# Block 1's tokens turned on VectorE and by DMA instead of on TensorE, the first loads reordered, and later sums moved to other places

## The chip, the cores and the metric

The kernel runs on one core of a Trainium2 chip. The core has five engines with an instruction queue each. TensorE (PE) multiplies matrices into PSUM. VectorE (DVE) and ScalarE (ACT) read and write PSUM and SBUF. GpSimd (POOL) works on SBUF alone. SyncE (SP) issues DMAs here, and ACT's queue issues some as well. Every queue is served in order: an instruction that waits holds up all those behind it on the same engine. The metric is the device time of one execution in microseconds (us).

## The reference

`x` is two samples of 2048 tokens with 512 features, `t` one condition vector of 512 for each sample. Everything is float32.

```python
emb = jnp.dot(jax.nn.silu(t), ada_w) + ada_b
shift_msa, scale_msa, gate_msa, shift_mlp, scale_mlp, gate_mlp = jnp.split(emb, 6, axis=-1)
norm = _ln(x) * (1.0 + scale_msa[:, None]) + shift_msa[:, None]
h = jax.nn.gelu(jnp.dot(norm, ssm_w1) + ssm_b1, approximate=False)
ssm_out = jnp.dot(h, ssm_w2) + ssm_b2
x = x + gate_msa[:, None] * ssm_out
norm2 = _ln(x) * (1.0 + scale_mlp[:, None]) + shift_mlp[:, None]
hf = jax.nn.gelu(jnp.dot(norm2, ff_w1) + ff_b1, approximate=True)
ff_out = jnp.dot(hf, ff_w2) + ff_b2
x = x + gate_mlp[:, None] * ff_out
```

`ssm_w1` and `ssm_w2` are 512x512, `ff_w1` is 512x1024, `ff_w2` 1024x512, and `ada_w` 512x3072, in six column groups `ada_0` to `ada_5`.

## The kernel before, in words

The 4096 tokens are cut into 8 blocks of 512 (`x_0` to `x_7`, 1 MB each). Each block goes through four stages: `hA` (the first ssm product and its gelu, class `First`), `oA` (the second ssm product, added into the block, `residual`), `hC` (first product of the feed-forward part, class `Second`) and `oC` (its second product). The stages of different blocks are interleaved by hand: after the start, PE's order is hA 0, oA 0, hA 1, oA 1, hC 0, hA 2, oC 0, hC 1 and so on, up to oA 6, hA 7, oC 5 and the end with block 7.

Each stage's product is done in the Strassen-Winograd way: seven products P1 to P7 of half-size matrices in place of eight, at the price of sums of the operands' quarters made beforehand (`sums_of_first`, `sums_of_second`: four operations s0, s1, a difference in place, and s2). A product is 8 matmuls of 128x128 with 256 columns. The seven gather in three PSUM banks: P1, P6, P7 and P4 share bank "y", P5 and P3 bank "v", P2 has "x". Every product that adds into a bank has to wait until the product before it in that bank has been read by DVE or ACT. The order of the seven is an argument: `ORDER` is P1 P2 P6 P5 P7 P3 P4, `FIRST` is P1 P2 P5 P6 P7 P3 P4, `CARRIED` is P1 P5 P6 P2 P7 P3 P4. The `hooks` of a stage are operations that are emitted after one of its products. They sit in the queues of their own engines in this order; with `CARRIED` the names of the places are those of `ORDER`, counted by position.

Before a block can be multiplied, it is normalized (mean and variance by `stats`, then `scales` on POOL, eight operations of four elements per partition, then `normal`), transposed so that features lie on partitions, and modulated with scale and shift. There are two ways of transposing. On PE: `turned` lets PE transpose 16 squares of 128x128 and modulates out of PSUM. By DVE and DMA: `turn` (DVE transposes 32x32 blocks, four operations), `move` (16 DMAs of 64 KB that carry the 32-row pieces between partitions) and `moved` (ACT modulates in place, four operations). Blocks 0 and 1 use PE for their first norm, all others the second way.

At the start SP issues the loads in the order x_0 (two halves), ada_0, ada_1, w1, ada_2, w2, the row of gate bias (`load_gate_b(2)`, four small DMAs), b2, x_1, ada_3, ada_4, fw1, and after block 0's first sums ada_5, fw2, `load_gate_b(5)`. The DMAs take eight semaphores in turn, so that each issue waits for the landing of the eighth DMA before it. `modulation(g0, part)` and `gate_rows_of(g)` multiply the condition with one ada group on PE (32 small matmuls into `pada`, line L275); DVE takes the result. `first_ssm_gate` spreads the ssm gate over the partitions (`pgate`, L310), and `fold2` multiplies w2 with it (four DVE operations, L396) and makes w2's four sums on POOL (L348). `seed` copies a bias row into a PSUM bank on ACT before the products add to it; block 0 has instead four POOL additions of the bias to `x_0` (`biases`, L752).

Of the kernel before, what the change touches and what calls it, by code (L numbers as in the profile page):

```python
# [36 lines left out]
F32 = mybir.dt.float32  # L37
# [103 lines left out]
def kernel(  # L141
# [16 lines left out]
    nc = tc.nc  # L158
# [100 lines left out]
    load_gate_b(2)  # L259
    b2_bc = work.tile([P, D], F32, tag="gb", name="gb2_0", bufs=2)  # L260
    load_row(b2_bc, b2)
    load_x(1)
    load_ada(3)
    load_ada(4)
    fw1_sb = load_w("fw1", fw1)

    mods = {}

# [224 lines left out]
    def hook(hooks, places, ops):  # L493

        for n, op in enumerate(ops):
            hooks.setdefault(places[min(n, len(places) - 1)], []).append(op)


    class Norm:
# [6 lines left out]
        def stats(self):  # L506
# [98 lines left out]
        def transpose(self, k, pt=None):  # L605
            if pt is None:
                pt = ps_t.tile([P, TB], F32, tag="t", name=f"pt{self.name}_{k}")
            for c in range(C):
                nc.tensor.transpose(
                    pt[:, c * P : (c + 1) * P], self.xn[:, c, k * P : (k + 1) * P], ident  # L610
                )
            return pt

# [31 lines left out]
        def summed(self, eng, in_big=False):  # L645

            if in_big:
                flat = big_tile(f"nS{self.name}").rearrange("p a b -> p (a b)")[:, : 3 * KD // 2 * HT]
                s = thirds(flat.rearrange("p (s a k r) -> p s a k r", s=3, a=C, k=KD // 2))
            else:  # L650
                s = thirds(sums.tile([P, 3, C, KD // 2, HT // C], F32, tag="s", name=f"nS{self.name}"))
            h = self.nT.rearrange("p a (k h r) -> p a k h r", k=KD, h=2)
            lo, hi = h[:, :, : KD // 2], h[:, :, KD // 2 :]
            q = {
                "11": lo[:, :, :, 0],
                "12": lo[:, :, :, 1],
                "21": hi[:, :, :, 0],
                "22": hi[:, :, :, 1],
            }
            self.ops = second_operands(q, s)  # L660
            return sums_of_second(q, s, eng)

    def hidden(name, rhs, wops, bT, func, lo, hi, g, hooks, order=ORDER, on_act=()):

# [262 lines left out]
    class First:  # L927
# [201 lines left out]
    load_ada(5)  # L1129
    fw2_sb = load_w("fw2", fw2)  # L1130
    load_gate_b(5)
    gb, hA = {2: b2_bc}, {}
    found = {}

# [8 lines left out]
        return [lambda k=k: found["w2"][1][k]() for k in range(lo, hi)]  # L1143

    hooks = {}
    hook(hooks, ("P1",), n1_sums[2:3])
    hook(hooks, ("P2",), [lambda: gate_rows_of(2, "grows")] + n1_sums[3:])
    st = n1[1].stats()
    hook(hooks, ("P5",), [ssm_gate, gb2_0] + biases(0, b2_bc) + [lambda: apart_row(b2_bc, nc.gpsimd)] + fold2(0, 1))
    hook(hooks, ("P6",), fold2(1, 7))  # L1150
    hook(hooks, ("P3", "P7"), st[:2])
    hook(hooks, ("P7",), [lambda: modulation(3, 0)])
    hA[0] = First(0, n1[0].ops, hooks, ("P1", "P2", "P5", "P6", "P3", "P7", "P4"), hA_0)
    w2_ops = found["w2"][0]

    hA_sums = hA[0].summed(nc.vector)
    run(hA_sums[:2])
    hooks = {}
    hook(hooks, ("P1",), hA_sums[2:3] + st[2:] + [n1[1].scales] + fold2(7, 8))
    hook(hooks, ("P2",), hA_sums[3:] + [lambda c=c: n1[1].normal(c, on_pe=True) for c in range(C)])  # L1160
    hook(hooks, ("P6",), [lambda: modulation(3, 1)])
    hook(hooks, ("P3", "P3", "P4"), n1[1].turned())
    n2 = {0: Norm(0, 2)}
    st = n2[0].stats()
    hook(hooks, ("P3",), st[:2])
    fw1_ops, fw1_sums, fw1_s = weight_of_first("fw1", fw1_sb)
    hook(hooks, ("P2",), fw1_sums[:1])
    hook(hooks, ("P5", "P4"), fw1_sums[1:3])
    residual("oA_0", 0, hA[0], w2_ops, KD // 2, hooks, order=FIRST)

    def ff_gate():
        take_gate(5, 0)
# [8 lines left out]


    n1_sums = n1[1].summed(nc.vector)
    run(st[2:3] + n1_sums[:2] + st[3:])
    hooks = {}
    hook(hooks, ("P1",), n1_sums[2:3] + [n2[0].scales])
    hook(hooks, ("P2",), n1_sums[3:] + [lambda c=c: n2[0].normal(c) for c in range(C)])
    hook(hooks, ("P5", "P7"), [lambda p=p: seed("oA_1", gb[2], p) for p in range(2)])
    hook(hooks, ("P6",), [lambda: gate_rows_of(5, "g5")])
    hook(hooks, ("P6", "P6", "P7", "P7"), [lambda c=c: n2[0].turn(c) for c in range(C)])  # L1190
    hook(hooks, ("P7",), [lambda: n2[0].move((nc.sync,), (0, 1)), lambda: store_gates(5), lambda: load_gate(5, 0)])
    fb2_bc = work.tile([P, D], F32, tag="gb", name="gb5_0", bufs=2)
# [85 lines left out]
    for i in range(1, NBLK):  # L1278
# [213 lines left out]
```

## Time and profile before

| what | value |
|---|---|
| time, median of 3 runs | 588.19 us (588.06 to 589.07) |
| the profiled execution's own time | 588.16 us |
| its span, first to last instruction | 586.4 us |
| PE busy | 577.9 us, 99% of the span |
| DVE, ACT, POOL busy | 417.9, 263.1, 428.4 us |
| mean granted TensorE clock | 0.999 |

The span is the time from the first to the last profiled instruction; 1.8 us of the time lie around it. A row of the timeline has the start, the length, the engine, the line in the kernel, the operation, output and input tiles, and in brackets the idle time of the engine just before and what ended it. Rows of one kind that follow each other are merged (x8 is eight instructions); the length of a merged matmul row is longer than the distance to the next row, since matmuls overlap: products of 8 follow each other every 1.73 us.

### The profile page before, as it was taken

Reading aid. Unit: us, or ns where it says so; the run is one execution under the profiler, and the core shown is the slowest. Engines: PE = TensorE matmul, PEld = TensorE weight load, DVE = VectorE, ACT = ScalarE, POOL = GpSimd, SP = SyncE. Lnnn points to the kernel's source line nnn. Section 1 sums busy time; section 2 is a strip of 40 time slices with the busy share of each in tenths; the row PEclk is TensorE's granted clock in tenths of the full one; section 3 lists DMA queues with packets and bytes.
Section 4 is the critical chain, followed back from the end, with each engine's and each line's share of the span. In section 5 each row is a group of like instructions: output and inputs, shape, how many; then the busy total and the mean of one; then the engine's idle time right before and its main releaser. Section 6 shows DMA issues by size and latency. Waiting matters only on the chain.

```text
span 586.4 us, 9484 instructions
## 1 busy us (share of the span) xinstructions
PE 577.9 (99%) x3303; PEld 515.5 (88%) x3303; DVE 417.9 (71%) x752; ACT 263.1 (45%) x479; POOL 428.4 (73%) x518
## 2 busy tenths in 40 slices
PE   8999999999999999999999999999999999999997
PEld 5888888888899888998889988898887998899896
DVE  4978788987867375685756857883856366787676
ACT  2234357405642554435742588226663431731420
POOL 2875359999997938969688799998688445369351
PEclk9999999999999999999999999999999999999999
DMA  8990323302205403472033721153030330031002
GB/s 317 395 393 10 91 64 82 108 37 107 55 19 178 129 1 74 113 209 72 3 90 78 282 73 29 45 141 129 19 72 1 106 113 0 1 73 72 2 1 72
DMA packets 25243, 56.49 MB, mean 96 GB/s; under 512 B 4672, under 2 KB 5740, under 8 KB 23532
## 3 DMA queue, kind: packets, MB, share of 16 engines
q1 hardware_dynamic: 21856, 51.67, 27.7%
q10 hardware_dynamic: 3340, 4.22, 3.0%
q8 instruction: 26, 0.43, 0.3%
q14 instruction: 21, 0.17, 0.1%
HBM read 32.80 MB, written 8.40 MB: 70 GB/s over the span
## 4 chain that ended last, share of the span: by engine, by line
PE 91%; DVE 3%; DMA 3%; issue 1%; ACT 0%; SPq 0%; DVEq 0%
PE px_hC L985 10%; PE py_hA L475 9%; PE py_oA L475 9%; PE py_hC L985 8%; PE py_oC L778 8%; PE pv_hC L985 8%; PE pl_oC_P_y L824 8%; PE pl_oC_P_v L824 5%; PE pv_hA L475 4%; PE pv_oA L475 4%; PE pl_oC_P_x L824 3%; DMA ada<-in_L_cond_ada_w_dram 2%; PE py_hC L475 2%; PE py_oC L475 2%; PE px_oA L475 2%; PE px_hA L475 2%
## 5 line engine op out<-in xcount | busy, mean ns | idle before, releaser
L623 ACT ACTIVATE nT<-nT,mod,mod 128x512 f32<-128x512 f32 x32 | 23.4, 803 | 56.2 <-DMA nT<-blocks 40.1
L348 POOL TENSOR_TENSOR hSC<-hClo,hChi 128x512 f32<-128x512 f32 (+1 forms) x16 | 19.7, 1235 | 38.7 <-ACT hChi L980 33.3
L512 DVE BATCH_NORM_STATS2 st<-x 128x6 f32<-128x512 f32 x60 | 40.7, 678 | 5.4 <-DMA x<-in_x_dram 5.2
L923 POOL TENSOR_TENSOR forms<-forms 128x256 f32<-128x256 f32 x56 | 41.8, 746 | 3.3
L985 PE MATMUL py_hC<-forms,fw 128*128 128x256 f32 x168 | 41.0, 380 | 0.0
L1002 DVE TENSOR_TENSOR hClo<-hClo,py_hC 128x512 f32<-128x512 f32 x42 | 28.6, 684 | 15.3 <-ACT hClo L999 9.4
L985 PEld LDWEIGHTS py_hC<-forms,fw 128*128 128x128 f32 x168 | 31.7, 190 | 4.7 <-DVE hClo L1002 0.2
L623 ACT ACTIVATE x<-x,mod,mod 128x512 f32<-128x512 f32 x24 | 17.6, 802 | 32.1 <-DMA x<-blocks 32.1
L591 DVE STREAM_TRANSPOSE blocks<-nT 128x512 f32<-128x512 f32 x32 | 22.2, 705 | 13.5 <-ACT nT L580 13.5
L923 POOL TENSOR_TENSOR forms<-nT,forms 128x256 f32<-128x256 f32 x42 | 30.5, 748 | 1.8 <-PE pl_oC_P_v L824 1.3
L923 POOL TENSOR_TENSOR forms<-nT 128x256 f32<-128x256 f32 x14 | 10.4, 740 | 29.3 <-ACT nT L623 20.4
L1002 DVE TENSOR_TENSOR hChi<-hChi,pv_hC 128x512 f32<-128x512 f32 x35 | 23.2, 681 | 10.4 <-PE pv_hC L985 6.7
L580 ACT ACTIVATE nT<-x,nmr,rstd 128x512 f32<-128x512 f32 x32 | 24.1, 806 | 13.4 <-POOL nmr L566 13.4
L985 PE MATMUL px_hC<-forms,fw 128*128 128x256 f32 x112 | 27.6, 379 | 0.0
L980 ACT ACTIVATE hClo<-hClo,colsT 128x256 f32<-128x256 f32 x56 | 25.3, 498 | 5.0 <-DVE hClo L1002 4.8
L838 DVE TENSOR_TENSOR x<-pl_oC_P_y,x 128x256 f32<-128x256 f32 (+1 forms) x66 | 24.7, 374 | 3.0 <-PE pl_oC_P_y L824 1.3
L475 PE MATMUL py_oA<-w,hA 128*128 128x256 f32 x112 | 26.5, 379 | 0.0
L999 ACT ACTIVATE hChi<-py_hC 128x512 f32<-128x512 f32 x14 | 7.6, 593 | 41.1 <-PE py_hC L985 41.0
L980 ACT ACTIVATE hChi<-hChi,colsT 128x256 f32<-128x256 f32 x56 | 25.1, 496 | 1.9 <-DVE hChi L1002 1.9
L739 DVE TENSOR_TENSOR x<-py_oA,x 128x512 f32<-128x512 f32 x26 | 17.8, 686 | 11.2 <-PE py_oA L475 10.6
L778 PE MATMUL py_oC<-fw_s,hSC 128*128 128x256 f32 x112 | 25.3, 379 | 0.0
L739 DVE TENSOR_TENSOR x<-pv_oA,x 128x512 f32<-128x512 f32 x16 | 11.0, 687 | 20.1 <-PE pv_oA L475 9.0
(339 smaller groups left out, 1796.7 us busy)
## 6 DMA issues: line engine op xcount, KB each, us to landing
x<-in_x_dram SPq DMA_DIRECT2D x13, 1024.0 KB
out_dram<-x SPq DMA_DIRECT2D x14, 512.0 KB
ada<-in_L_cond_ada_w_dram SPq DMA_DIRECT2D x6, 1024.0 KB
x<-blocks SPq DMA_DIRECT2D x96, 64.0 KB
nT<-blocks SPq DMA_DIRECT2D x80, 64.0 KB
fw<-in_L_cond_ff_w_dram SPq DMA_DIRECT2D x2, 2048.0 KB
w<-in_L_cond_ssm_w_dram SPq DMA_DIRECT2D x3, 1024.0 KB
nT<-blocks ACTq DMA_DIRECT2D x48, 64.0 KB
```

The lines of the kernel that those rows point to most:

```text
L475: nc.tensor.matmul(ps[b][j * apart][:, j, :], lhs(p, j, k), rhs(p, j, k), start=(fresh and j * (not apart) == 0 and k == 0), stop=(p in (" ...
L512: nc.vector.bn_stats(st, xs[self.i][:, c, :])
L580: nc.scalar.activation(t, x_c, AF.Identity, bias=self.nmr[:, c : c + 1], scale=self.rstd[:, c : c + 1])
L623: nc.scalar.activation(dst, src, AF.Identity, bias=shift, scale=scale)
L739: nc.vector.tensor_tensor(d, ps[BANK[p]][:, js], d, ALU.add)
L778: yield lambda j=j, k=k: nc.tensor.matmul(ps[BANK[p]][:, j, :], hops(p, j, k), wops[p][:, k, :], start=False, stop=(k == kdim - 1), skip_g ...
L824: nc.tensor.matmul(t[:, n, :], hops.leaves[p][f][:, k, :], leaf_wops[p][f][:, k, :], start=room not in started, stop=(f in ("P2", "P3", "P ...
L838: nc.vector.tensor_tensor(d, src, d, ALU.add)
L923: eng.tensor_tensor(reg[d], reg[a], reg[b], ALU.add if f == "+" else ALU.subtract)
L980: nc.scalar.activation(h, h, AF.Gelu_apprx_tanh, bias=fb1T[:, m : m + 1])
L985: nc.tensor.matmul(ps[b][:, j, :], fa[ra][:, j * P : (j + 1) * P], fb[rb].rearrange("p a (c q) -> p c a q", q=Q), start=(fresh and j == 0) ...
L1002: nc.vector.tensor_tensor(dest(d), dest(d), ps[b], op)
```

## The change

Six things are done. First, `x_1` is loaded right behind `w1`, fw1 comes ahead of ada_3, and ada_4, ada_5, fw2, gate bias 5 are issued behind block 1's moves. Second, block 1 is turned by DVE and DMA: its statistics are taken half by DVE and half by ACT (`stats_shared`) during hA 0, the normals run on ACT, and the moves are issued on SP and ACT at the end of hA 0. Third, block 0's ssm bias is seeded into PSUM; the four POOL additions go. Fourth, in hA 0 the gate's products come after P5 and not after P2, two biases of the hidden layer are added on ACT, three of the four sums of its output go to POOL, and the modulation 3 leaves hA 0 for oA 0 and hA 1; oA 0 runs in `ORDER` in place of `FIRST`. Fifth, the sums of fw1, of block 0's second norm and the folds of fw2 stand at other places or engines. Sixth, for the last block (`ahead`) the four sums of the first norm are made after the fourth and the fifth product of oA 6 and after the first and second of hA 7; before, two came after the third product of oA 6, one after the fourth and one after the fifth. The transposes of block 0 on PE are written as matmuls that open their PSUM bank once.

```diff
     w1_sb = load_w("w1", w1)
+    load_x(1)
     load_ada(2)
...
     load_row(b2_bc, b2)
-    load_x(1)
+    fw1_sb = load_w("fw1", fw1)
     load_ada(3)
-    load_ada(4)
-    fw1_sb = load_w("fw1", fw1)
...
+        def stats_shared(self):
...
+            def on_dve(c):
...
+                nc.vector.bn_stats(st, xs[self.i][:, c, :])
+                nc.vector.bn_aggr(self.mv[:, c, :], st)
+
+            def mean(c):
+                nc.scalar.activation(
+                    unread[:, c], xs[self.i][:, c, :], AF.Identity, scale=1.0 / D, accum_out=self.mv[:, c, :1]
+                )
+
+            def square(c):
+                nc.scalar.activation(
+                    unread[:, c],
+                    xs[self.i][:, c, :],
+                    AF.Square,
+                    bias=less[:, c : c + 1],
+                    scale=half,
+                    accum_out=self.mv[:, c, 1:],
+                )
+
+            first, second = [range(h * C // 2, (h + 1) * C // 2) for h in range(2)]
+            rest = slice(C // 2, C)
+            return [lambda c=c: mean(c) for c in second] + [lambda c=c: on_dve(c) for c in first], [
+                lambda: nc.gpsimd.tensor_scalar(less[:, rest], self.mv[:, rest, 0], -half, None, ALU.mult)
+            ] + [lambda c=c: square(c) for c in second]
...
-        def summed(self, eng):
+        def summed(self, eng, first=None):
...
-            return sums_of_first(q, s, eng)
+            return sums_of_first(q, s, first or eng)[:1] + sums_of_first(q, s, eng)[1:]
...
+    st, squares = n1[1].stats_shared()
+    normals = [lambda c=c: n1[1].normal(c) for c in range(C)]
+    turns = [lambda c=c: n1[1].turn(c) for c in range(C)]
+    hook(hooks, ("P1",), st)
+    hook(hooks, ("P2",), squares + [n1[1].scales] + n1_sums[2:3])
+    hook(hooks, ("P5",), [lambda: gate_rows_of(2, "grows")] + n1_sums[3:])
+    hook(hooks, ("P6",), [ssm_gate, gb2_0, lambda: apart_row(b2_bc, nc.gpsimd)] + fold2(0, 2) + normals)
+    hook(hooks, ("P6", "P4"), [lambda p=p: seed("oA_0", b2_bc, p) for p in range(2)])
+    hook(hooks, ("P7",), turns[:2] + fold2(2, 5))
+    hook(hooks, ("P3",), turns[2:3] + fold2(5, 6))
+    hA[0] = First(0, n1[0].ops, hooks, FIRST, hA_0, ("P1", "P5"))
+    w2_ops = found["w2"][0]
+
+    hA_sums = hA[0].summed(nc.gpsimd, nc.vector)
+    run(hA_sums[:1])
+    n1[1].turn(3)
+    n1[1].move((nc.sync, nc.scalar))
+    load_ada(4)
     load_ada(5)
     fw2_sb = load_w("fw2", fw2)
     load_gate_b(5)
...
-    hook(hooks, ("P1",), n1_sums[2:3])
-    hook(hooks, ("P2",), [lambda: gate_rows_of(2, "grows")] + n1_sums[3:])
-    st = n1[1].stats()
-    hook(hooks, ("P5",), [ssm_gate, gb2_0] + biases(0, b2_bc) + [lambda: apart_row(b2_bc, nc.gpsimd)] + fold2(0, 1))
-    hook(hooks, ("P6",), fold2(1, 7))
-    hook(hooks, ("P3", "P7"), st[:2])
-    hook(hooks, ("P7",), [lambda: modulation(3, 0)])
-    hA[0] = First(0, n1[0].ops, hooks, ("P1", "P2", "P5", "P6", "P3", "P7", "P4"), hA_0)
...
-    run(hA_sums[:2])
+    run(hA_sums[1:2] + fold2(6, 7) + hA_sums[2:])
     hooks = {}
-    hook(hooks, ("P1",), hA_sums[2:3] + st[2:] + [n1[1].scales] + fold2(7, 8))
-    hook(hooks, ("P2",), hA_sums[3:] + [lambda c=c: n1[1].normal(c, on_pe=True) for c in range(C)])
-    hook(hooks, ("P6",), [lambda: modulation(3, 1)])
-    hook(hooks, ("P3", "P3", "P4"), n1[1].turned())
+    hook(hooks, ("P1",), fold2(7, 8))
+    hook(hooks, ("P6",), n1[1].moved())
...
+    hook(hooks, ("P4",), [lambda: modulation(3, 0)])
...
-    hook(hooks, ("P5", "P4"), fw1_sums[1:3])
-    residual("oA_0", 0, hA[0], w2_ops, KD // 2, hooks, order=FIRST)
+    hook(hooks, ("P5",), fw1_sums[1:2])
+    residual("oA_0", 0, hA[0], w2_ops, KD // 2, hooks)
...
-    run(st[2:3] + n1_sums[:2] + st[3:])
+    run(st[2:] + n1_sums[:2])
...
+    hook(hooks, ("P1", "P6"), [lambda: modulation(3, 1), lambda: gate_rows_of(5, "g5")])
...
-    hA[1] = First(1, n1[1].ops, hooks, FIRST)
+    hA[1] = First(1, n1[1].ops, hooks, FIRST, on_act=("P1",))
...
-    n2_sums = n2[0].summed(nc.gpsimd)
-    hook(hooks, ("P5",), n2_sums[:1] + [n1[2].scales])
-    hook(hooks, ("P7",), n2_sums[1:] + [lambda c=c: n1[2].normal(c) for c in range(C)])
-    hook(hooks, ("P7", "P3", "P4"), fold5(0, 3))
+    n2_sums = n2[0].summed((nc.vector, nc.vector, nc.gpsimd, nc.gpsimd))
+    hook(hooks, ("P5",), [n1[2].scales])
+    hook(hooks, ("P7",), n2_sums + [lambda c=c: n1[2].normal(c) for c in range(C)])
+    hook(hooks, ("P7",), fold5(0, 1))
...
             if ahead:
-                hook(hooks, ("P6", "P6", "P5", "P7"), n1[i + 2].summed(nc.vector, True))
+                n1_sums = n1[i + 2].summed(nc.vector, True)
+                hook(hooks, ("P5", "P7"), n1_sums[:2])
...
             if ahead:
                 hooks = {}
+                hook(hooks, ("P1", "P2"), n1_sums[2:])
                 hook(hooks, ("P2", "P6"), oC_seeds)
```

More of the change, by code (lines that the diff above doesn't have):

```diff
@@ L515, in stats @@
             return [lambda c=c: op(c) for c in range(C)]
+        def stats_shared(self):
+            n, half = self.name, D**-0.5
+            self.mv = small.tile([P, C, nc.vector.BN_AGGR_DIM], F32, tag="mv", name=f"mv{n}")
+            unread = work.tile([P, C, D], F32, tag="blocks", name=f"unread{n}")
+            less = small.tile([P, C], F32, tag="less", name=f"less{n}", bufs=1)
+            def on_dve(c):
+                st = small.tile([P, nc.vector.BN_STATS_DIM], F32, tag="st", name=f"st{n}_{c}")
+                nc.vector.bn_stats(st, xs[self.i][:, c, :])
[18 more added lines that the diff above has]
+            ] + [lambda c=c: square(c) for c in second]
         def sums_on_act(self):
@@ L608, in transpose @@
             for c in range(C):
-                nc.tensor.transpose(
-                    pt[:, c * P : (c + 1) * P], self.xn[:, c, k * P : (k + 1) * P], ident
+                nc.tensor.matmul(
+                    pt[:, c * P : (c + 1) * P],
+                    self.xn[:, c, k * P : (k + 1) * P],
+                    ident,
+                    start=(c == 0),
+                    stop=(c == C - 1),
+                    is_transpose=True,
+                    skip_group_check=True,
                 )
@@ L660, in summed @@
             self.ops = second_operands(q, s)
-            return sums_of_second(q, s, eng)
+            engs = eng if isinstance(eng, tuple) else (eng,) * 4
+            return [sums_of_second(q, s, e)[n] for n, e in enumerate(engs)]
     def hidden(name, rhs, wops, bT, func, lo, hi, g, hooks, order=ORDER, on_act=()):
@@ L1128 @@
     run(n1_sums[:2])
-    load_ada(5)
-    fw2_sb = load_w("fw2", fw2)
-    load_gate_b(5)
     gb, hA = {2: b2_bc}, {}
@@ L1145 @@
     hooks = {}
-    hook(hooks, ("P1",), n1_sums[2:3])
-    hook(hooks, ("P2",), [lambda: gate_rows_of(2, "grows")] + n1_sums[3:])
-    st = n1[1].stats()
-    hook(hooks, ("P5",), [ssm_gate, gb2_0] + biases(0, b2_bc) + [lambda: apart_row(b2_bc, nc.gpsimd)] + fold2(0, 1))
-    hook(hooks, ("P6",), fold2(1, 7))
-    hook(hooks, ("P3", "P7"), st[:2])
-    hook(hooks, ("P7",), [lambda: modulation(3, 0)])
-    hA[0] = First(0, n1[0].ops, hooks, ("P1", "P2", "P5", "P6", "P3", "P7", "P4"), hA_0)
-    w2_ops = found["w2"][0]
-    hA_sums = hA[0].summed(nc.vector)
-    run(hA_sums[:2])
+    st, squares = n1[1].stats_shared()
[9 more added lines that the diff above has]
+    hA[0] = First(0, n1[0].ops, hooks, FIRST, hA_0, ("P1", "P5"))
+    w2_ops = found["w2"][0]
+    hA_sums = hA[0].summed(nc.gpsimd, nc.vector)
[3 more added lines that the diff above has]
+    load_ada(4)
+    load_ada(5)
+    fw2_sb = load_w("fw2", fw2)
+    load_gate_b(5)
+    run(hA_sums[1:2] + fold2(6, 7) + hA_sums[2:])
     hooks = {}
-    hook(hooks, ("P1",), hA_sums[2:3] + st[2:] + [n1[1].scales] + fold2(7, 8))
-    hook(hooks, ("P2",), hA_sums[3:] + [lambda c=c: n1[1].normal(c, on_pe=True) for c in range(C)])
-    hook(hooks, ("P6",), [lambda: modulation(3, 1)])
-    hook(hooks, ("P3", "P3", "P4"), n1[1].turned())
+    hook(hooks, ("P1",), fold2(7, 8))
+    hook(hooks, ("P6",), n1[1].moved())
     n2 = {0: Norm(0, 2)}
@@ L1183 @@
     n1_sums = n1[1].summed(nc.vector)
-    run(st[2:3] + n1_sums[:2] + st[3:])
+    run(st[2:] + n1_sums[:2])
     hooks = {}
-    hook(hooks, ("P1",), n1_sums[2:3] + [n2[0].scales])
-    hook(hooks, ("P2",), n1_sums[3:] + [lambda c=c: n2[0].normal(c) for c in range(C)])
+    hook(hooks, ("P1",), n1_sums[2:3] + [n2[0].scales] + fw1_sums[2:])
+    hook(hooks, ("P2",), [lambda c=c: n2[0].normal(c) for c in range(C)])
     hook(hooks, ("P5", "P7"), [lambda p=p: seed("oA_1", gb[2], p) for p in range(2)])
-    hook(hooks, ("P6",), [lambda: gate_rows_of(5, "g5")])
+    hook(hooks, ("P1", "P6"), [lambda: modulation(3, 1), lambda: gate_rows_of(5, "g5")])
     hook(hooks, ("P6", "P6", "P7", "P7"), [lambda c=c: n2[0].turn(c) for c in range(C)])
+    hook(hooks, ("P6",), n1_sums[3:])
     hook(hooks, ("P7",), [lambda: n2[0].move((nc.sync,), (0, 1)), lambda: store_gates(5), lambda: load_gate(5, 0)])
@@ L1205 @@
     hooks = {}
-    hook(hooks, ("P1",), hA_sums[2:3] + fw1_sums[3:])
+    hook(hooks, ("P1",), hA_sums[2:3])
     hook(hooks, ("P2",), hA_sums[3:])
@@ L1224 @@
     hook(hooks, ("P3",), [n2[1].scales])
-    hook(hooks, ("P6", "P5", "P7", "P3", "P4"), fold5(3, 8))
+    hook(hooks, ("P2", "P6", "P5", "P7", "P3", "P4"), fold5(1, 8))
     hook(hooks, ("P4",), [lambda: store_gates(2)])
```

## The prediction

> **What bounds the kernel now.** The page's first part says PE is busy 99% of the span, so only PE's own work and its few waits count. The waits by engine name PE's in the program's body, the chain of waits and PE's timeline place them, and DVE's timeline says why the last one arises. Waits of PE, longest first:
>
> ```profile
> PE py_oA L475 <- DVE x L739: 1.4, 1, 1.4
> PE idle L1078 <- POOL ident masks.py:199: 1.3, 1, 1.3
> PE rowsT L1087 <- DMA fw_t<-in_L_cond_ff_b_dram: 0.7, 1, 0.7
> PE pada L275 <- DMA ada<-in_L_cond_ada_w_dram: 0.7, 2, 0.4
> ```
>
> The first sits in the last blocks; the next two lie ahead of all that is changed. PE's timeline at the start (16 to 29 us), at block 1's transposes and around the long wait:
>
> ```profile
> 16.47 1.89 PE L475 MATMUL px_hA<-nT,w 128*128 128x256 f32 x8
> 18.60 1.08 PE L275 MATMUL pada<-ada,silu 128*32 128x128 f32 x32 [0.25 <-DMA ada<-in_L_cond_ada_w_dram]
> 19.61 1.99 PE L475 MATMUL pv_hA<-nS,w_s 128*128 128x256 f32 x8
> 21.45 1.05 PE L310 MATMUL pgate<-grows,fw_t 128*128 128x128 f32 x8
> 27.61 1.08 PE L275 MATMUL pada<-ada,silu 128*32 128x128 f32 x32
> ...
> 42.19 1.04 PE L609 MATMUL pt<-ident,blocks 128*128 128x128 f32 x8
> 43.06 1.89 PE L475 MATMUL py_oA<-w_s,forms 128*128 128x256 f32 x8
> 44.79 1.04 PE L609 MATMUL pt<-ident,blocks 128*128 128x128 f32 x8
> ...
> 439.55 1.89 PE L475 MATMUL pv_oA<-w,hSA 128*128 128x256 f32 x8
> 442.83 1.99 PE L475 MATMUL py_oA<-w_s,hA 128*128 128x256 f32 x8 [1.39 <-DVE x L739]
> 444.66 1.67 PE L475 MATMUL py_hA<-x,w 128*128 128x256 f32 x7
> ```
>
> A product of 8 takes 1.73 us, start to start. From 439.55 to 442.83 it is 3.28: PE stands 1.55 us ahead of P4 of oA 6. DVE's timeline there:
>
> ```profile
> 437.32 1.50 DVE L348 TENSOR_TENSOR nS<-x 128x512 f32<-128x512 f32 x1 [0.26 <-ACT x L623]
> 438.93 1.57 DVE L348 TENSOR_TENSOR nS<-x,nS 128x512 f32<-128x512 f32 x1
> 440.42 0.68 DVE L739 TENSOR_TENSOR x<-px_oA,x 128x512 f32<-128x512 f32 x1
> 441.02 1.16 DVE L348 TENSOR_TENSOR x<-x 128x512 f32<-128x512 f32 x1
> 442.10 0.68 DVE L739 TENSOR_TENSOR x<-py_oA,x 128x512 f32<-128x512 f32 x1
> ```
>
> P4 goes into the bank that P7 filled by 439.7, and P7's read (442.10) stands behind three of block 7's sums. Nothing else between 46 and 570 us keeps PE waiting.
>
> **The change part by part.** Times are those of the profiled execution (588.16 us, 0.03 under the median of 588.19).
>
> *Transposes gone.* Two groups of 8 (42.19, 44.79) push the products after them by 0.87 and 0.88 us (chain of waits: 42.35 to 43.23, 44.96 to 45.83): -1.75.
>
> *x_1 ahead of ada_2.* SP's timeline issues x_1 at 14.54, ada_3 at 18.58 and ada_4 at 21.27; its waits there are for w1, ada_2 and w2, the eighth DMA before each. So w1 lands at 14.5, ada_2 at 18.56, w2 at 21.26. A megabyte at the page's 395 GB/s takes 2.66; ada_2 took 4.0, and 1.35 of that is a delay that the later loads carry on. With x_1 in between, ada_2 gets about w2's place. Bounds: 14.5 + 2 x 2.66 = 19.85 without the delay, 21.26 with it. I take 21.2, nearest to the row that shows the second place. Now PE's P2 ends at 18.20 and pada starts at 18.60, a wait of 0.40. Then P1, P2 and P5 end at 19.93 and pada waits until 21.25, 1.32: +0.92 (bounds -0.40 and +0.98). x_1 itself comes at 18.5.
>
> *hA 0 afterwards*, PE: pada to 22.26, P6 to 24.18 (1.92 behind a pada, as at 19.68), pgate to 25.07, P7 to 26.80, P3 to 28.53, P4 to 30.26. The 0.16 that PE stands at 28.6 behind DVE's folds go with the new order: -0.16.
>
> *ACT.* Two means (0.61 each from the rows of block 6's first norm, line L524) after x_1 end at 19.8, the table load (1.28) at 21.1, P2's gelu at 21.7, two squares (0.72, L535) at 23.1. P5's biases (0.84) cost nothing, as P3 reads that bank at 26.8. POOL's scales (3.03 from 35.97 to 39.00) end at 26.2, four normals (2.93) at 29.2, the seed (0.57) at 29.8, before P1 of oA 0 at 30.26. So the seed costs nothing; if x_1's chain comes later it does, from 0.5 us on.
>
> *DVE.* The two bn_stats wait for x_1 to 18.5 and end at 20.2; P2's add waits behind them, but its gelu is first used at 30.26. The gate's rows wait for pada, which is there at 22.3. From pgate at 25.2 on DVE has nine operations in a row, 0.60 apart: b2's product, two folds, P7's add, two turns, two folds, P3's add, ending at 30.7. Then ACT's gelu of P3 (0.55) and P4 (0.84) at 32.15. P2 of oA 0 needs P4's, and could have started at 31.99: +0.2 (bounds 0, and 2.0 if two of the nine take 1.5 like 437.32).
>
> *POOL.* Its four bias additions (4.97 in a row) vanish and relieve nothing that PE waits for. New there are hA 0's three sums, between w2's. From 32.1 on: s1 33.4 (P6 wants it at 33.9), w2's and hA's difference 36.0 (P7: 37.4), s2 37.3 (P3: 39.1), w2's s2 38.6 (P4: 40.8), at 1.27 each. Nothing at 1.27; at 1.72, as beside DVE's sums at 31 us, each still comes, with 0.1 to spare.
>
> *Moves.* The last turn ends at 32.7. 16 issues run on SP and ACT, eight each: 5.05 and 5.2 in the rows of block 0's moves. ACT went on 1.66 after the last issue, here at 39.5; the four modulates end at 42.4. ACT stands still for 7 us, which costs nothing, as oA 0 asks nothing of it. hA 1 starts at 45.83 - 0.8 - 1.2 (a pada group with its edge moves behind it) = 43.85 and needs the first two modulates, at 41.0: spare 2.8.
>
> *Loads behind the moves.* SP issues ada_4 at 37.8. x_0's first half took 4.0 for 512 KB, so a megabyte takes 5.3 at most: 43.1. PE wants it at 45.6, spare 2.5. ada_5 45.8, fw2 51.1, gate bias 5 about 51.5 against DVE's need at 53.0. x_2 at 55 is read at 61. fw1, in ada_3's former place, is there before 30; POOL uses it from 39.
>
> *Later sums.* fw1's, block 0's second norm's and the folds of fw2 move among POOL and DVE in stages where PE has no wait. The nearest need is s1 of n2 0 on PE at 74.5, made on DVE by 69: nothing.
>
> *Block 7's sums.* DVE reads P2 at 438.0 (436.10 + 1.89), makes s0 (1.5) to 440.15, reads P7 to 440.85. P4 can start on time at 441.28, spare 0.4. s1 ends at 442.4, wanted at 446.5; the in-place difference at 448.3, wanted at 449.9. -1.55 (bounds -1.55 and -0.9, the rest a 0.65 slip of s0).
>
> Sum: -1.75 + 0.92 - 0.16 + 0.2 - 1.55 = -2.34, 588.16 to 585.8; the 1.8 us around the span stay. Within 0.2% (1.2 us) a measurement of this kernel can't be told from no change.
>
> A rule that speaks against it: by the Trainium skill, TensorE: Matmul & The Clock Gate, Part 1, an idle window of about 3.4 us puts PE back to half clock. Here the windows show a granted clock of 1.00 from the start to 582 us and 0.83 only in the last 4.4, with PE done; the new wait of 1.3 is below it, and at half clock the next 3.4 us would cost an estimated 1.7 more. And by ScalarE: Activation LUTs, What ACT_TABLE_LOAD costs, the table load in ACT's new chain would take about 2.7 us; the rows have 1.28 each time, and with 2.7 the normals would end 1.4 later and the seed would hold P1 up by an estimated 0.9.
>
> **The rivals.** *ada_2 without the delay:* the delay of 1.35 might fall elsewhere. For it: w1 and x_0 had none. Against: it starts at about 17 us, whatever is loaded then. Wait 0, so 0.40 gained in place of 0.92 lost: 584.5. Chance 0.1.
>
> *Block 1's chain is tight:* x_1 to means, squares, scales, normals, turns, folds, P3, P4 runs through four engines in order, and POOL's sums follow with 0.5 spare. For it: DVE and POOL rows of 1.5 to 1.7 when both read SBUF. Against: DVE's nine are mostly reads of PSUM. It costs 0.8 to 1.9 more: 586.6 to 587.7, say 587.0. Chance 0.2, half of it within 0.2%.
>
> *Block 7's wait only moves,* to P4 still or to P7 of hA 7: spare 0.4 and 1.6. Then 0.8 of the start is all: 587.4. Chance 0.06.
>
> *Slower: block 1's tokens come late.* hA 1 waits for the last move. It has 2.8 spare and 2.34 gained, so it decides against the change by 0.2% only if the last turn ends 6.3 later than 32.7, at 39.0; each us beyond that is one us more, and at 40.5 the time is 590.8. For it: turns, moves and ada_4 stand behind each other, and a normal that waits holds ACT, DVE's folds and the gelus. Against: the chain summed from rows has no gap of that size. Chance 0.09.
>
> **How the numbers follow.** The forecast case has 0.55: 585.8, own range 585.2 to 586.4. Faster: 0.55 + 0.1 + 0.1 = 0.75, and 0.01 of block 7's case: 0.76; same: 0.1 + 0.04: 0.14; slower: 0.09 and 0.01 of that case: 0.1. The range from 584.4 to 587.8 holds all but the slower case.
>
> **What would show it.** No L609 after 15 us; one pada wait near 21 with ada_2 as releaser; a gap under 0.5 ahead of oA 0's P2; hA 1 near 43.9; no wait in oA 6. It is wrong if PE waits for ACT's modulates at hA 1, for a pada at 45, or for DVE around 441.

## The result and the profile after

The changed kernel takes 585.89 us (median of 6 runs, 585.66 to 586.95) against 588.21 us before (588.06 to 589.07): ratio 0.9963, 95% interval 0.9951 to 0.9975. It is 0.4% faster, clear of the noise, and the forecast was 585.8. The profiled execution took 585.66, against 588.16 for the one of before: 2.50 less. All sums below are made between these two.

The span and the first part of the page of the changed kernel, and PE's waits in the program's body (line, tile, what released it, us in total, times, longest):

```profile
span 583.8 us, 9508 instructions
PE 577.3 (99%) x3287; PEld 514.4 (88%) x3287; DVE 411.9 (71%) x748; ACT 269.0 (46%) x495; POOL 424.6 (73%) x516
```

```profile
PE idle L1117 <- POOL ident masks.py:199: 1.3, 1, 1.3
PE pada L274 <- DMA ada<-in_L_cond_ada_w_dram: 1.0, 1, 1.0
```

The wait of 1.4 for DVE in oA 6 is gone. The wait for `ada_2` has grown. PE's timeline of the changed kernel shows where (start, length, engine, line, operation; products of 8 follow each other every 1.73):

```profile
18.27 1.89 PE L474 MATMUL pv_hA<-nS,w_s 128*128 128x256 f32 x8
21.13 1.08 PE L274 MATMUL pada<-ada,silu 128*32 128x128 f32 x32 [0.98 <-DMA ada<-in_L_cond_ada_w_dram]
...
23.98 1.05 PE L309 MATMUL pgate<-grows,fw_t 128*128 128x128 f32 x8
25.01 1.97 PE L474 MATMUL py_hA<-nT,w 128*128 128x256 f32 x8
...
30.27 1.89 PE L474 MATMUL py_oA<-w,forms 128*128 128x256 f32 x8
31.99 1.89 PE L474 MATMUL px_oA<-w,forms 128*128 128x256 f32 x8
...
43.46 1.99 PE L474 MATMUL py_hA<-nT,w 128*128 128x256 f32 x8
...
438.67 1.89 PE L474 MATMUL pv_oA<-w,hSA 128*128 128x256 f32 x8
440.39 1.89 PE L474 MATMUL py_oA<-w_s,hA 128*128 128x256 f32 x8
```

Each price is read as a distance between starts. P5 should end at 18.27 + 1.73 = 20.00, and `pada` starts at 21.13: a wait of 1.13, where before there was one of 0.40. From `pgate` to the next product (P7 now, P6 before) it is 1.03 instead of 0.89: P7 adds into the bank of P6, and DVE's read of P6 starts at 24.18, takes 0.69 and ends 0.14 before P7 starts. P1 and P2 of oA 0 follow without a gap, and hA 1 starts at 43.46. From P3 to P4 of oA 6 it is 1.72: nothing is left of the 1.55 there. The account against the profiled execution of before:

| step | forecast | measured |
|---|---|---|
| 16 transposes of block 1 gone from PE | -1.75 | -1.75 |
| wait for `ada_2` | +0.92 | +0.73 |
| the 0.16 behind DVE's folds gone | -0.16 | -0.16 |
| P2 of oA 0 behind P4's gelu | +0.2 | 0 |
| `pgate` to the next product | none | +0.14 |
| block 7's sums | -1.55 | -1.55 |
| start of hA 0 (14.76 for 14.68) | none | +0.08 |
| sum | -2.34 | -2.51 |

The chain of block 1 on ACT ran as it was added up. ACT's timeline of the changed kernel, with the table load, the four normals, the seed and the four modulates:

```profile
19.81 1.28 ACT L734 ACT_TABLE_LOAD   x1
...
26.45 2.93 ACT L612 ACTIVATE nT<-x,nmr,rstd 128x512 f32<-128x512 f32 x4 [2.59 <-POOL nmr L598]
29.29 0.57 ACT L446 COPY py_oA<-gb 128x512 f32<-128x512 f32 x1
...
40.75 2.93 ACT L661 ACTIVATE nT<-nT,mod,mod 128x512 f32<-128x512 f32 x4 [8.11 <-DMA nT<-blocks]
```

The normals end at 29.4 (forecast 29.2) and the seed at 29.86 (29.8), 0.4 before P1 of oA 0. The table load was to take 1.28 by the rows of before, and it does: it runs from 19.81 to 21.09, and the next ACTIVATE starts at 21.10. The Trainium skill, ScalarE: Activation LUTs, What ACT_TABLE_LOAD costs, makes up its 2.7 of 1.28 for the load and 1.38 for a drain. The load's part agrees with the row, the drain's is not seen here. DVE's timeline of the changed kernel, first in hA 1, then around the old wait in oA 6:

```profile
53.37 0.29 DVE L302 TENSOR_TENSOR grows<-pada,fw_t 128x128 f32<-128x128 f32 x1 [0.80 <-DMA fw_t<-in_L_cond_ada_b_dram]
...
55.37 0.68 DVE L740 TENSOR_TENSOR hA<-py_hA,hA 128x512 f32<-128x512 f32 x1
...
437.14 0.69 DVE L778 TENSOR_TENSOR x<-px_oA,x 128x512 f32<-128x512 f32 x1 [0.96 <-PE px_oA L474]
437.75 1.53 DVE L347 TENSOR_TENSOR nS<-x 128x512 f32<-128x512 f32 x1
439.20 0.68 DVE L778 TENSOR_TENSOR x<-py_oA,x 128x512 f32<-128x512 f32 x1
```

In oA 6, P7's read at 439.20 now stands behind one sum of block 7 in place of three; it ends at 439.88, 0.5 before P4 wants the bank. In hA 1 there is something that the prediction had not: DVE stands 0.80 until gate bias 5 has landed (53.2). In e9, where it lands early, DVE stands 0.35 there, for PE, and goes on at 52.91. So gate bias 5 comes about 0.5 too late, where the forecast had it 1.5 early. DVE's read of P7 (L740) then ends at 56.05, 0.3 before P4 of hA 1 starts (56.34). This does not cost anything in this execution, but the spread of the runs (1.3 us, where e9 has 0.2) comes from here.

### The profile page after: what moved, and what is told of

It reads as the page before. It is cut to its first block, busy times and chain, and to the rows that moved or that the text cites. A ratio compares the mean times of both kernels' runs of the same rounds, so it can differ in the third digit from the quotient of the medians.

```text
span 583.8 us, 9508 instructions
## 1 busy us (share of the span) xinstructions
PE 577.3 (99%) x3287; PEld 514.4 (88%) x3287; DVE 411.9 (71%) x748; ACT 269.0 (46%) x495; POOL 424.6 (73%) x516
## 4 chain that ended last, share of the span: by engine, by line
PE 94%; DMA 3%; DVE 2%; issue 0%; ACTq 0%; DVEq 0%
PE px_hC L1024 10%; PE py_oA L474 9%; PE py_hA L474 9%; PE py_hC L1024 8%; PE py_oC L817 8%; PE pv_hC L1024 8%; PE pl_oC_P_y L863 8%; PE pv_oA L474 5%; PE pl_oC_P_v L863 5%; PE pv_hA L474 4%; PE pl_oC_P_x L863 3%; DMA ada<-in_L_cond_ada_w_dram 3%; PE px_oA L474 2%; PE py_oC L474 2%; PE py_hC L474 2%; PE px_hA L474 2%
## 5 line engine op out<-in xcount | busy, mean ns | idle before, releaser
L661 ACT ACTIVATE nT<-nT,mod,mod 128x512 f32<-128x512 f32 x36 | 26.4, 803 | 63.4 <-DMA nT<-blocks 57.2
L511 DVE BATCH_NORM_STATS2 st<-x 128x6 f32<-128x512 f32 x56 | 37.9, 677 | 5.1 <-DMA x<-in_x_dram 4.9
L623 DVE STREAM_TRANSPOSE blocks<-nT 128x512 f32<-128x512 f32 x36 | 24.9, 703 | 13.5 <-ACT nT L612 13.5
L612 ACT ACTIVATE nT<-x,nmr,rstd 128x512 f32<-128x512 f32 x36 | 27.0, 805 | 13.5 <-POOL nmr L598 13.5
L580 POOL TENSOR_SCALAR ve<-mv 128x4 f32<-128x4 f32 x16 | 3.7, 234 | 39.2 <-DVE mv L512 36.8
L1038 ACT ACTIVATE hClo<-px_hC 128x512 f32<-128x512 f32 x21 | 12.5, 596 | 28.1 <-PE px_hC L1024 23.2
```

The lines of the kernel that those rows point to most:

```text
L511: nc.vector.bn_stats(st, xs[self.i][:, c, :])
L612: nc.scalar.activation(t, x_c, AF.Identity, bias=self.nmr[:, c : c + 1], scale=self.rstd[:, c : c + 1])
L623: nc.vector.transpose(self.bl[:, :, :, c, :].rearrange("p m k q -> p k m q"), self.nT[:, c, :].rearrange("p (k m q) -> p k m q", k=KD, m=C),)
L661: nc.scalar.activation(dst, src, AF.Identity, bias=shift, scale=scale)
```

## The experiments

Theory: PE is the bound, and the time follows the gaps on PE one for one; the gain is 1.75 from the transposes and 1.55 from block 7's sums, and the order "x_1, then ada_2" pays for it with a wait. Rivals: the sums or the transposes were hidden anyway; the `ada_2` wait could be had for nothing by another order; the four bias additions on POOL matter, which the prediction denied; the moves are late. "After" is the changed kernel, "before" ran beside each (588.2 each time).

**e1: after, with block 7's sums in their old places.**

```diff
-                n1_sums = n1[i + 2].summed(nc.vector, True)
-                hook(hooks, ("P5", "P7"), n1_sums[:2])
+                hook(hooks, ("P6", "P6", "P5", "P7"), n1[i + 2].summed(nc.vector, True))
...
-                hook(hooks, ("P1", "P2"), n1_sums[2:])
```

> The changed kernel with block 7's four sums put back to their old places in oA 6. Theory (the terms of the sum add up): PE waits again about 1.5 us ahead of P4 of oA 6, released by DVE's read of P7, and the time is 585.9 + 1.55 = 587.4. Rival (the wait went because everything ahead of it moved, or its microseconds are given back later): no wait over 0.5 us there, or 585.9 in spite of it.

Measured: 588.16 (587.24 to 589.37, 11 runs), ratio to before 1.0 (0.9991 to 1.0008). The profiled execution, 587.24, is 1.58 above that of after. PE's timeline of e1 has the old wait back, 1.55 beyond the pitch (441.89 - 438.61 = 3.28):

```profile
438.61 1.89 PE L474 MATMUL pv_oA<-w,hSA 128*128 128x256 f32 x8
441.89 1.99 PE L474 MATMUL py_oA<-w_s,hA 128*128 128x256 f32 x8 [1.39 <-DVE x L778]
```

The wait and its place are shown. The median rose by 2.27, more than the 1.58 of the profiles; the spread is 2.1 us here and 1.3 in after. Why it is larger here stays open.

**e2: before, with block 7's sums alone in their new places** (the edit of e1 turned round).

> The kernel before with nothing changed but block 7's four sums, spread over oA 6 and hA 7. Theory: the wait of 1.55 us at 441 us goes, 588.2 - 1.55 = 586.65, and the start is as before. Rival (the sums only move the wait, to P7 of hA 7 or to the last block): 588.2.

Measured: 586.61 (586.5 to 586.72, 7 runs), ratio 0.9973 (0.9962 to 0.9984): 1.6 gained, and in PE's timeline of e2 P4 of oA 6 follows P3 by 1.73:

```profile
439.63 1.89 PE L475 MATMUL pv_oA<-w,hSA 128*128 128x256 f32 x8
441.36 1.89 PE L475 MATMUL py_oA<-w_s,hA 128*128 128x256 f32 x8
```

So this part is worth the same alone and with the rest. All the rest of the change together, at the start of the kernel, is then worth 0.7 by the medians (586.61 to 585.89) and 0.95 by the profiled executions.

**e8: after, with 16 transposes on PE again.** They are put where they stood before; their result is read by nobody, so this kernel does work beyond the reference's.

```diff
+    def unread_transposes(n):
+        t = ps_t.tile([P, TB], F32, tag="t", name=f"unread_t_{n}")
+        for c in range(2 * C):
+            nc.tensor.transpose(t[:, c % C * P : (c % C + 1) * P], ident, ident)
+
+    hook(hooks, ("P3", "P4"), [lambda n=n: unread_transposes(n) for n in range(2)])
     residual("oA_0", 0, hA[0], w2_ops, KD // 2, hooks)
```

> The changed kernel with 16 transposes of 128x128 that nobody reads put back into PE's stream in oA 0, where block 1's stood. Theory (their whole time was on the path): 585.9 + 1.75 = 587.65. Rival (hA 1 has to wait for the modulates anyway, or the transposes only fill time that PE stands idle): 585.9 to 586.5.

Measured: 587.44 (587.19 to 587.82, 11 runs), ratio 0.9985 (0.9977 to 0.9994); profiled 587.27, 1.61 above after's. PE's timeline of e8:

```profile
40.70 1.04 PE L1217 MATMUL unread_t<-ident 128*128 128x128 f32 x8
41.58 1.89 PE L474 MATMUL py_oA<-w_s,forms 128*128 128x256 f32 x8
...
44.41 1.09 PE L1217 MATMUL unread_t<-ident 128*128 128x128 f32 x8
45.34 1.89 PE L474 MATMUL py_hA<-nT,w 128*128 128x256 f32 x8
```

They push what follows by 0.88 and 0.93. At the start of oA 1, 1.78 of that is still there (59.84 for 58.06), and 1.65 from 346 us on. So PE's time is the path here, and next to nothing of the transposes was hidden.

**e3: after, with `ada_2` loaded ahead of `x_1`, as before.**

```diff
-    load_x(1)
     load_ada(2)
+    load_x(1)
```

> The changed kernel with ada_2 loaded ahead of x_1. ada_2 lands near 18.4 and PE's wait of 1.13 us for it goes; x_1 lands near 21.1, 2.7 later. Theory (block 1's chain from x_1 through ACT, POOL and DVE ends with almost nothing to spare): normals end near 32.0 and the seed of oA 0 near 32.5, where PE stands from 29.2 on, so 3.3 are lost for 1.1 gained: 588.1, with PE waiting for ACT at oA 0's start. Rival (the chain has spare, and PE's wait for ada_2 is the whole loss): 584.8.

Measured: 588.86 (588.66 to 589.43, 11 runs), ratio 1.0013 (1.0004 to 1.0022). It is slower than before, and the 1.13 for `ada_2` is gone. PE's timeline of e3 shows what came in its place:

```profile
20.00 1.08 PE L274 MATMUL pada<-ada,silu 128*32 128x128 f32 x32
21.01 1.99 PE L474 MATMUL py_hA<-nS,w_s 128*128 128x256 f32 x8
24.28 1.16 PE L309 MATMUL pgate<-grows,fw_t 128*128 128x128 f32 x8 [1.28 <-DVE grows L302]
...
29.10 1.89 PE L474 MATMUL py_hA<-nS,w 128*128 128x256 f32 x8
32.47 1.99 PE L474 MATMUL py_oA<-w,forms 128*128 128x256 f32 x8 [1.48 <-ACT py_oA L446]
```

`x_1` lands at 21.1 in place of 18.4, 2.7 later. The gate's rows on DVE stand behind the statistics that wait for it, and the seed on ACT stands behind the normals. The two gaps are 24.28 - 21.01 - 1.83 = 1.44 and 32.47 - 29.10 - 1.72 = 1.65; P4 of hA 1 has a third of 0.67, behind gate bias 5, which lands at 56.4 here. Less the 1.13 saved they make 2.6 of the 3.1 between the two profiled executions; most of the rest is in the distances right after these waits (from `pgate` to P7 1.29 for 1.03). So `x_1` first is right, and block 1's chain stands close behind the `ada_2` wait. With clock 1.00 in all of it, a wait of 1.65 did not touch the clock.

**e4: after, with the gate's rows behind P6 and its product, the folds and the seed behind P7, so that PE needs `ada_2` one product later.**

```diff
-    hook(hooks, ("P5",), [lambda: gate_rows_of(2, "grows")] + n1_sums[3:])
-    hook(hooks, ("P6",), [ssm_gate, gb2_0, lambda: apart_row(b2_bc, nc.gpsimd)] + fold2(0, 2) + normals)
-    hook(hooks, ("P6", "P4"), [lambda p=p: seed("oA_0", b2_bc, p) for p in range(2)])
+    hook(hooks, ("P5",), n1_sums[3:])
+    hook(hooks, ("P6",), [lambda: gate_rows_of(2, "grows")] + normals)
+    hook(hooks, ("P7",), [ssm_gate, gb2_0, lambda: apart_row(b2_bc, nc.gpsimd)] + fold2(0, 2))
+    hook(hooks, ("P7", "P4"), [lambda p=p: seed("oA_0", b2_bc, p) for p in range(2)])
```

> The changed kernel with the gate's rows computed after P6 and the gate spread after P7 in hA 0, so that PE no longer waits for ada_2; x_1 and the normals as they are. Theory (block 1's chain on ACT and DVE is as late as PE's wait makes it): the wait for ada_2 goes, but P1 of oA 0 then waits for the seed, which stands behind the normals until 29.9 and P7's gelu, to about 30.4, and P2 for P4's gelu to about 32.1: 585.9 to 586.1, nothing gained. Rival (PE's wait was a pure loss): 585.9 - 1.1 = 584.8.

Measured: 586.0 (585.74 to 586.64, 5 runs), ratio 0.9965 (0.9953 to 0.9978), as good as after. PE's timeline of e4:

```profile
27.24 1.89 PE L474 MATMUL py_hA<-nS,w 128*128 128x256 f32 x8
30.31 1.99 PE L474 MATMUL py_oA<-w,forms 128*128 128x256 f32 x8 [1.18 <-ACT py_oA L446]
...
57.26 1.99 PE L474 MATMUL py_hA<-nS,w 128*128 128x256 f32 x8 [0.61 <-DVE hA L740]
```

The 1.13 at `ada_2` is gone and 1.34 at oA 0 has come: P1 starts at 30.31, in after at 30.27. P1's start is set by ACT's chain x_1, means, squares, normals, seed, and what PE does in the meantime is free. The second gap (57.26 - 54.76 - 1.73 = 0.77) is DVE's again: it waited 1.81 us, most of it for gate bias 5, which landed at 54.4 in this execution. SP's eight move issues took 6.71 us here and 5.31 in after's profile, so the loads behind them went out 1.2 later, and gate bias 5 landed 1.2 later. That is the spread, caught in a profile.

**e9: after, with gate bias 5 loaded ahead of `fw2` (2 MB).**

```diff
-    fw2_sb = load_w("fw2", fw2)
     load_gate_b(5)
+    fw2_sb = load_w("fw2", fw2)
```

> The changed kernel with the four small loads of gate bias 5 issued ahead of fw2 and not behind it. Theory (what varies from run to run in the changed kernel is when gate bias 5 lands behind fw2: DVE's gate rows in hA 1 wait for it, 0.8 us in the profile shown and 1.8 in that of the kernel with the late gate, and P7's read stands behind them with 0.3 to spare): that wait goes, PE waits for nothing after ada_2, and the times gather at 585.7 with a spread of 0.3. Rival (the spread comes from the moves, or from somewhere else): median 585.9 and still up to 587.

Measured: 585.63 (585.55 to 585.77, 5 runs), ratio 0.9953 (0.9941 to 0.9966). DVE's timeline of e9 has the gate rows released by PE and no longer by a DMA:

```profile
52.91 0.29 DVE L302 TENSOR_TENSOR grows<-pada,fw_t 128x128 f32<-128x128 f32 x1 [0.35 <-PE pada L274]
```

The spread fell from 1.3 to 0.2. The order of these two loads let the time vary in after.

**e10: e9 and e4 together, and the chain cleared:** the seed and P7's gelu ahead of the normals, two normals behind P4's gelu, the folds ahead of the turns, and all four turns behind the first sum of hA 0's output.

```diff
...
+    hook(hooks, ("P5",), n1_sums[3:])
+    hook(hooks, ("P6",), [lambda: gate_rows_of(2, "grows")])
+    hook(hooks, ("P7",), [ssm_gate, gb2_0, lambda: apart_row(b2_bc, nc.gpsimd)] + fold2(0, 2))
+    hook(hooks, ("P7", "P4"), [lambda p=p: seed("oA_0", b2_bc, p) for p in range(2)])
+    hook(hooks, ("P7",), normals[:2])
+    hook(hooks, ("P3",), fold2(2, 6))
+    hook(hooks, ("P4",), normals[2:])
...
-    run(hA_sums[:1])
-    n1[1].turn(3)
+    run(hA_sums[:1] + turns)
...
```

> The changed kernel with gate bias 5 ahead of fw2, the gate's rows after P6 and the gate spread after P7 (no wait for ada_2), and block 1's chain made shorter where it holds PE: the seed and P7's gelu ahead of the normals on ACT, two of the normals behind P4's gelu, w2's folds ahead of the turns on DVE. Theory (PE's wait for ada_2 and the chain on ACT and DVE are two waits behind one another, and only both together are worth 1.1): P1 of oA 0 starts near 29.2, P2 near 30.9, hA 1 near 42.4 where the modulates just suffice: 584.7 to 585.0. Rival (a third one is right behind: moves or ada_4): 585.7.

Measured: 585.44 (585.26 to 585.66, 5 runs), ratio 0.9951 (0.9937 to 0.9964); 0.4 more than the upper end of what was expected, because of a new wait. PE's and DVE's timelines of e10:

```profile
30.58 1.89 PE L474 MATMUL px_oA<-w,forms 128*128 128x256 f32 x8
33.29 1.96 PE L474 MATMUL py_oA<-w_s,hSA 128*128 128x256 f32 x8 [0.81 <-DVE x L778]
```

```profile
29.80 2.77 DVE L623 STREAM_TRANSPOSE blocks<-nT 128x512 f32<-128x512 f32 x4
32.49 0.65 DVE L778 TENSOR_TENSOR x<-py_oA,x 128x512 f32<-128x512 f32 x1
```

P1 of oA 0 moved from 30.27 to 28.86, but P6 had to wait 0.98 for DVE's read of P1, which stood behind the four turns.

**e11: e10, with two of the turns, the moves and the loads behind DVE's read of P1.**

```diff
-    run(hA_sums[:1] + turns)
-    n1[1].move((nc.sync, nc.scalar))
-    load_ada(4)
-    load_ada(5)
-    load_gate_b(5)
-    fw2_sb = load_w("fw2", fw2)
+    run(hA_sums[:1] + turns[:2])
...
-    hook(hooks, ("P1",), fold2(7, 8))
+    hook(hooks, ("P1",), turns[2:] + [moves_and_loads] + fold2(7, 8))
```

(`moves_and_loads` issues the five removed operations in the order shown.)

> The kernel with the shorter chain and the early gate bias, and two of block 1's four turns moved behind DVE's read of P1 in oA 0, with the moves and the loads after them issued there. In the run with the shorter chain PE waited 0.98 us ahead of P6 of oA 0 for that read, which stood behind all four turns. Theory: the read ends near 31.8, P6 starts on time near 32.3, the moves start 0.4 later, and hA 1 starts near 42.3 with at most 0.3 of wait for the modulates: 584.6 to 584.9. Rival (the moves' landing is as late as PE's wait made it): PE waits for ACT's modulates at hA 1 and the time stays at 585.4.

Measured: 584.61 (584.34 to 585.2, 5 runs), ratio 0.9941 (0.9927 to 0.9954), the fastest of all. PE's waits in e11:

```profile
PE idle L1117 <- POOL ident masks.py:199: 1.3, 1, 1.3
PE rowsT L1126 <- DMA fw_t<-in_L_cond_ff_b_dram: 0.4, 1, 0.4
PE pada L274 <- DMA ada<-in_L_cond_ada_w_dram: 0.3, 1, 0.3
```

All three lie before 13 us. hA 1 starts at 42.43 instead of 43.46. So the 1.13 for `ada_2` was not needed, but to be rid of it was worth something only when the waits behind it had been cleared too: the seed (e4 against e10) and the read of P1 (e10 against e11), both with gate bias 5 early. The five runs of e11 still spread by 0.9; what varies there is not shown.

**e6: after, with four POOL additions of block 0's bias in place of the seeds.** The prediction said that these additions "relieve nothing that PE waits for".

```diff
-    hook(hooks, ("P6",), [ssm_gate, gb2_0, lambda: apart_row(b2_bc, nc.gpsimd)] + fold2(0, 2) + normals)
-    hook(hooks, ("P6", "P4"), [lambda p=p: seed("oA_0", b2_bc, p) for p in range(2)])
+    hook(hooks, ("P6",), [ssm_gate, gb2_0] + biases(0, b2_bc) + [lambda: apart_row(b2_bc, nc.gpsimd)] + fold2(0, 2) + normals)
```

> The changed kernel with block 0's bias added on POOL again (four operations of 1.24) in place of the two seeds. Theory (the seeds are what makes room on POOL, since w2's and hA 0's sums stand there one behind another): w2's sums start 5.0 later, hA 0's s1 ends near 35.9, and PE's P6 of oA 0, ready at 33.7, waits 2.2: 588.1. Rival, as the prediction had it (the four additions relieve nothing that PE waits for): 585.9.

Measured: 590.1 (588.59 to 590.29, 6 runs), ratio 1.0025 (1.0014 to 1.0037): 2.0 more than the 588.1 that was expected. POOL's and PE's timelines of e6, then its table of windows (window, its length, busy time and instructions of PE, PEld, DVE, ACT, POOL, granted clock, DMA share, GB/s):

```profile
26.39 4.99 POOL L791 TENSOR_TENSOR x<-x,gb 128x512 f32<-128x512 f32 x4
...
35.23 1.26 POOL L347 TENSOR_TENSOR hSA<-hSA,forms 128x512 f32<-128x512 f32 x1
```

```profile
36.54 3.10 PE L474 MATMUL py_oA<-w_s,hSA 128*128 128x256 f32 x8 [2.70 <-POOL hSA L347]
39.43 2.51 PE L474 MATMUL pv_oA<-w_s,hSA 128*128 128x256 f32 x8
41.78 1.89 PE L474 MATMUL py_oA<-w,forms 128*128 128x256 f32 x8
```

```profile
36.00:38.00 2.00, 1.46 (x5) 1.29 (x6) 0.00 (x0) 0.00 (x0) 2.00 (x3) 0.82 0.40 93
38.00:40.00 2.00, 2.00 (x6) 1.55 (x6) 0.32 (x1) 0.00 (x0) 2.00 (x2) 0.50 0.84 190
40.00:42.00 2.00, 2.00 (x10) 1.68 (x8) 0.37 (x1) 0.92 (x2) 2.00 (x3) 0.83 0.91 173
```

The additions take 4.99 on POOL, the sum s1 that P6 needs comes at 36.5, and PE waits 2.86 beyond the pitch. After that the granted clock is 0.50 for 3.4 us, and P6 and P5 take 2.89 and 2.35 in place of 1.73 each: 1.78 more. 2.86 + 1.78 = 4.64, against 4.61 between the profiled executions. So the step of the prediction falls: with hA 0's sums on POOL, its four additions have no room. One run of the six, 588.59, was 1.5 below the median. It has no profile, but its mean granted clock is 0.999, where the five others have 0.995 to 0.997: it fits that the clock stayed up in it and the wait alone was paid (585.66 + 2.86 = 588.52).

**e7: after, with all 16 moves on SP.**

```diff
-    n1[1].move((nc.sync, nc.scalar))
+    n1[1].move((nc.sync,))
```

> The changed kernel with all 16 moves of block 1 issued by SP. SP needs 0.66 to 0.8 for one, so the last lands 5 to 6.5 later than now, near 45.6 to 47.1. Theory (the prediction's slower case: hA 1 waits for the moves, one for one beyond a spare of 1.2 in place of the 2.8 forecast): PE waits 3.6 to 5.3 at hA 1, released by ACT's modulates; a wait of that length also halves PE's clock for the next matmuls, as 2.9 us did in the run with the bias on POOL, 1.7 more: 591 to 592.7. Rival (spare 2.8, and no clock effect): 588 to 589.5.

Measured: 590.5 (590.23 to 591.5, 5 runs), ratio 1.0044 (1.0032 to 1.0057). SP's and PE's timelines of e7 and one of its windows:

```profile
32.81 10.53 SPq L632 DMA_DIRECT2D nT<-blocks  x16
```

```profile
42.34 1.08 PE L274 MATMUL pada<-ada,silu 128*32 128x128 f32 x32
45.93 3.21 PE L474 MATMUL py_hA<-nT,w 128*128 128x256 f32 x8 [2.50 <-ACT nT L661]
49.06 1.76 PE L274 MATMUL pada<-ada,silu 128*32 128x128 f32 x32
```

```profile
48.00:50.00 2.00, 2.00 (x23) 1.20 (x25) 1.29 (x2) 0.83 (x2) 1.75 (x5) 0.50 1.04 395
```

The last move landed at 44.8 in place of 40.6. 4.2 later cost a wait of 2.58 (45.93 less 42.34 and the 1.01 that after has there), so after's spare at hA 1 is 1.6. Then the clock halves again: hA 1's P1 takes 3.13 for 1.92 and the next `pada` 1.70 for 1.01, 1.9 more; some 0.2 of that is P1's third matmul, which starts only at 46.64, behind ACT's second modulate. 2.58 + 1.9 is 4.5 of the 4.57 between the profiles. This is the prediction's slower rival, made to happen by way of the moves: a wait of 2.6 cost 4.5. The other four runs have mean granted clocks from 0.993 to 0.999 and no profile, so how the time is shared there is open.

## Why the prediction was right, and where its steps were not

*Transposes gone, -1.75:* right. e8 brings back 0.88 and 0.93.

*x_1 ahead of ada_2, +0.92:* the place and releaser were right, the size was 0.73. `ada_2` came at 21.1, as taken from w2's row, so the delay of 1.35 stayed with the second load; the rival without it (584.5) is out. `pada` could start at 21.13 for 21.25, and P5 ended at 20.00 for 19.93. e3 shows that the other order costs 3 us, e4 that ACT's chain holds PE for 1.34 when the wait for `ada_2` is gone.

*Chain of block 1 through four engines:* right to 0.2 up to the turns (POOL's scales 26.4 for 26.2, normals 29.4 for 29.2, s1 33.5 for 33.4, last turn 32.76 for 32.7). The tight-chain rival did not happen, but e3, e4 and e10 show how near it stood: the seed had 0.4 spare, and each relief met a next wait of 1.0 to 1.65 us.

*P2 behind P4's gelu, +0.2:* wrong by 0.2. P2 started at 31.99, while the gelu, two instructions, ended at 32.15. So its first matmuls did not need the second of them.

*"Nothing" for POOL's additions:* this step failed. It asked only whether PE had waited for them before. In the new order they would have kept PE waiting 2.86 for hA 0's sums (e6). The change's sum was right because the additions do go; the reason given for the price was not.

*Moves landed at 39.5, spare 2.8:* mis-sized. They landed at 40.6, and e7 measures a spare of 1.6. Of the last move's 16 parts 15 had landed at 39.8; the last one made it 40.6.

*Loads behind the moves:* mis-sized. `ada_4` was issued at 38.3 for 37.8 and took 6.3, where the prediction had 5.3 "at most": 14 of its 16 parts had landed at 43.6, the last at 44.6 for 43.1. Its spare was 0.8 and not 2.5. Gate bias 5, behind it, landed at 53.2 for "about 51.5". The lag of a load's last part, a delay that the prediction itself said later loads carry on, was left out of these lines (that it explains the whole is argued; what e9 shows is that the place behind `fw2` matters). In after the late gate bias cost 0 to 1.3 us from run to run.

*Block 7's sums, -1.55:* right; e1 and e2 show it from both sides, with 0.5 spare (forecast 0.4).

*The slower rival, "one us more each":* its price was too low, as e7 shows: the wait brought half clock behind it, 1.9 on top of 2.58.

*The sum:* that it comes within 0.1 of the median is partly luck. Two terms were too high by 0.39 together (`ada_2` 0.19, P2 of oA 0 0.2), 0.22 was not forecast at all (the product behind `pgate` 0.14, the start 0.08), and the median stands 0.23 above the profiled execution because of gate bias 5, which the prediction took to be early.

## What to carry to other kernels

Where one engine is busy 99% of the span, add up its row-to-row distances and follow each new wait's queue to the next one: relief at the first wait is worth only the spare at the second (e4 gained nothing; e11, with the next waits cleared as well, one us). Ask of each operation that is moved away what the freed room is now used for, not whether anybody had waited for it before. Where times spread, look for a small load behind a large one that somebody waits for: here a swap of two loads took the spread from 1.3 to 0.2.

## What the hardware showed that was not expected

The clock fell after shorter stops than the prediction had allowed for. PE stood for 1.13, 1.55 and 1.65 beyond its pitch in after, e1 and e3, and the clock stayed at 1.00. It stood for 2.58 and 2.86 in e7 and e6, and the clock went to 0.50 for 3.4 us each time, beginning about 1.2 and 0.7 after PE had gone on. The Trainium skill, TensorE: Matmul & The Clock Gate, Part 1, gives an idle window of about 3.4 us before half clock. The length of the slow stretch agrees with that window, but here stops of 2.6 to 2.9 were enough; where between 1.65 and 2.58 the limit lies, no run shows. The length of a stop may not be all that counts: in the traces of e6 and e7 every whole stretch between two changes of the clock is a multiple of 3.41 us (3.41 slow, then 546.13 and 535.89 at full clock, 160 and 157 times as long), so the clock changes on a fixed grid. In the 3.41 us just before it fell, PE had stood for 2.7 (e6) and 2.2 (e7). Whether a stop's place on the grid decides was not tested.

From about 16 us on, one of the 16 parts of each load lands about 1.3 us behind the others, and a load counts as landed only with its last part: 15 parts of `x_1` had landed at 17.1, the last at 18.4, when SP went on. In the trace's DMA packets one of 16 KB from an instruction queue (q8) starts just then (16.3 before, 16.1 after, 1.1 us long). That this packet holds up one of the engines fits the times; the trace does not say which engine took it, and it was not tested. Why SP's eight move issues took 5.31 us in after's profile and 6.71 in e4's, with the same code, stays open as well.
